# Loading a group's residual among the steps before it, and joining turned planes one sub-step later

## The chip, the cores and the metric

The kernel runs on one core of a Trainium2 chip. The metric is the time of one execution in device microseconds (us). The core has five instruction queues that run beside each other: TensorE (PE: matmuls, and PEld for its weight loads), VectorE (DVE), ScalarE (ACT), GpSimd (POOL) and SyncE (SP), which here issues nearly all DMAs. Each engine takes its instructions strictly in the order in which they were compiled, so an instruction that waits holds up everything behind it on its engine.

## The reference

The input x is 8 sequences of 2048 tokens of 256 features, in fp32. Three residual sublayers follow each other:

```python
x = x + 0.5 * ffn(layernorm(x), w1, b1, w2, b2)
x = x + s4d(layernorm(x), log_A_real, A_imag, C_re, C_im, log_dt, D, ln_w, ln_b)
x = x + 0.5 * ffn(layernorm(x), w1, b1, w2, b2)
```

```python
def ffn(x, w1, b1, w2, b2):              # width 1024
    h = relu(einsum('bsd,dw->bsw', x, w1) + b1)
    return einsum('bsw,wd->bsd', h, w2) + b2

def s4d(x, ...):                         # a long convolution for each of the 256 features
    K = s4d_kernel(log_A_real, A_imag, C_re, C_im, log_dt, length)
    y = irfft(rfft(x) * rfft(K))[:length]
    r = x + y + x * D
    return layernorm(r) * ln_w + ln_b    # over the features
```

The kernel K of the convolution is a sum over 64 complex exponentials for each feature. It depends on the parameters alone, not on x.

## The kernel before

**Stages.** The kernel runs the first feed-forward ("a", up to some 820 us), then the convolution in blocks of 128 tokens (some 820 to 1010 us), then the second feed-forward ("b"). The work that this case is about lies in the first feed-forward. Beside it, the tables of the convolution are computed: the generator `matrices()` makes them, and they need nothing of the feed-forward.

**The feed-forward.** It is cut into 64 groups of 256 tokens, and each group into 8 steps. `sublayer` runs a loop over steps; step t does for group t // 8 one slice of 128 of the 1024 hidden features: six matmuls into the PSUM tile `ph` (`up`, L856; six, because fp32 operands are split into a high and a low part), a relu on ACT that gives the high part (L928), and an instruction on DVE that gives the low part of the same slice (`stt`, recorded as L116, output `hx`). Three steps later (LAG = 3) six matmuls of `down` (L866) add that slice into `po`. So PE needs from ACT and DVE one `hx` for each step. Four `hx` buffers and four `ph` banks lie between them.

**Before a group** (`pre_a`, started 18 steps ahead of its first matmul, one `yield` for each step): its residual is loaded into one of five buffers `x` (L983, one DMA of 256 KB on SP's queue), four steps later (XY = 4) DVE takes its statistics (L693, `st_fa`), ACT normalizes it into `xn` (L730), and it is transposed, either on PE (L794, then ACT L803 and DVE L805) or, in groups 14 to 18 and 44 on, through DRAM by DMA (L815 to L837). Groups 0 to 2 are loaded seven steps later than the others (XL = 7).

**After a group** (`post_a`): DVE adds `po` to the residual (L992), SP stores the result as `x1` (L993), DVE takes its statistics (`st_u`, L693) and ACT writes its normalized form into `u` in two halves (L730, `u`). The statistics of group g are finished together with those of group g + 3 in small instructions of four columns (a `Joint`; `t_u`, `q_u`, `nb_u`, recorded at L714, L116 and L717). The second half of `u` is the last reader of the residual, which then frees its buffer for the load of group g + 5.

**The tables.** `matrices()` ends in a loop over 32 batches; in iteration bt four parts are advanced together through six sub-steps, each part by one `yield` for each sub-step:

- `make(bt)`: POOL computes the batch's matrix P in six instructions of 128x512 (L600 to L610), in one of four buffers, which the batch four before must have left.
- `spread(bt - 1)`: ACT splits P into two planes of 16 bits (L620, two copies), SP stores the planes in DRAM (L623, `pv`) and P itself (L625, `o`).
- `turn(bt - 2)`: SP loads the planes back with a DMA that transposes them (L631).
- `transpose(bt - 3)`: after PY sub-steps the two turned planes are joined to fp32 again, one by DVE and one by ACT (L646, "the join"), in the buffer where P was; a sub-step later SP stores the result (L650, `pt`), and the buffer is free when that store has landed.

There are two buffers of planes, used in turn. The sub-steps are paced beside the steps: a step advances the clock of the feed-forward by 1.32, a sub-step that of the tables by 9.1 / 6 or 10.3 / 6. The work of `lags` (L536 to L570 on POOL, PE and DVE) is advanced in the same loop.

**What sets the order.** The Python code gives an order of calls; a scheduler with a model of time then orders each engine's instructions, except those marked `keep_in_program_order`, which stay in order among themselves. The joins, the turning DMAs and the pinned copies are so marked. A change of one call can therefore move other instructions some places on their engines.

Of the kernel before, what the change touches and what calls it, by code (L numbers as in the profile page):

```python
# [19 lines left out]
P = 128  # L20
# [23 lines left out]
def macaron_s4d_kernel(  # L44
# [17 lines left out]
    nc = tc.nc  # L62
# [4 lines left out]
    B, L, H = x.shape  # L67
# [8 lines left out]
    NTB = 2  # L76
    TOK = NTB * P
    NG = NJ * B // NTB
# [33 lines left out]
    def slot(tag, shape, name, dtype=F32):  # L112
        return work.tile(shape, dtype, name=name, tag=tag, bufs=BUFS[tag])
# [144 lines left out]
    def matrices():  # L258
# [73 lines left out]
        f, a = r, z  # L332
# [29 lines left out]
        for k in range(1, 4):  # L362
# [14 lines left out]
        er, qr, qi, den, ta, tb, c2r, c2i, cr, ci, aa, ab, big, fa, fb, v, s, tt, g, e, mm_ = (  # L377
            cells[18:39]
        )
# [86 lines left out]
        for i in range(H // P):  # L466
            nc.gpsimd.dma_start(
                out=kpad[i * P : (i + 1) * P, P + 1 :], in_=zeros[:, 0 : P - 1]
# [6 lines left out]
        with nc.allow_non_contiguous_dma(reason="256 numbers"):  # L475
            nc.gpsimd.dma_start(
                out=kpad.rearrange("(g c) k -> c g k", c=2)[:, :, P], in_=k0
# [100 lines left out]
        def p_of(bt):  # L578

            r, i = (room[2], 28 + bt % 4 * 8) if bt < first else (room[3], (16, 24, 48, 56)[bt % 4])  # L580
            return r[:, i * P : (i + 8) * P]
# [57 lines left out]
        def transpose(bt):  # L639
            pl, ptb = planes[:, bt % 2], p_of(bt)  # L640
            for _ in range(PY):
                yield
# [9 lines left out]

        planes = wpool.tile([P, 2, 2, BCH * P], U16, name="planes", tag="wE")
        P_REINT = (V.tensor_copy, A_.copy)
        PY = 0
        BACK = 3
        DI = 2
        PX = 2
# [79 lines left out]
    def hbm(ap, g):  # L738
        j, b0 = g // GPJ, g % GPJ * NTB
        return ap[b0 : b0 + NTB, j * P : (j + 1) * P, :].rearrange("b p h -> p b h")  # L740
# [220 lines left out]
    xts = {}  # L961
# [14 lines left out]
    JG = 3  # L976

    def pre_a(g):
        by_dma = g >= DMA_A and not DMA_X <= g < DMA_Y
        for _ in range(XL if g < JG else 0):  # L980
            yield
        xt = xts[g] = slot("x", [P, NTB, H], f"xa_{g}")
        nc.sync.dma_start(out=xt, in_=hbm(x, g))  # L983
        for _ in range(XY):
            yield
        if g >= JG:
            joints[g - JG] = Joint(g - JG, by_dma)
        return (yield from ffn_in(xt, f"a{g}", NTB, by_dma, joints.get(g - JG)))
# [229 lines left out]
    def begin():  # L1218
        for _ in range(sizes[1] // PB):
            next(head)  # L1220

    sublayer(
        w1t, w2t, pre_a, post_a, 18, "a", load_weights(), chain(matrices(), early()),
        {"half": NG // 2, "tables": NG * 3 // 4},
        {NG * SLOTS - 6: lambda: next(head), NG * SLOTS - 1: begin},
# [127 lines left out]
```

## Time and profile before

| | |
|---|---|
| time, median of 3 runs | 1777.33 us (1776.58 to 1781.38) |
| the profiled execution | 1773.09 us, of which its span is 1771.3 us |
| PE busy | 1729.9 us, 98% of the span |
| DVE busy | 1373.3 us, 78% |
| ACT busy | 997.8 us, 56% |
| POOL busy | 591.5 us, 33% |
| joins (L646) | 32 on DVE, median 846 ns, from 248.1 to 602.6 us; 32 on ACT, median 1371 ns |
| residual loads (L983) | 64, 256 KB each, median 3.1 us from issue to landing |
| turning DMAs (L631) | 32, median 5.8 us from issue to landing |

Shares are means over the whole span, and the stages differ. In the rows of the profile, "x" before a number is a count of instructions. A group is named by its line, engine and operation and by what it writes and reads (`hx_a<-ph_a`). A bracket after a row, or a row of the waits, tells how long the engine had stood idle and what ended that. PEclk is the granted share of PE's clock.

### The profile page before, as it was taken

To read this page: it belongs to the slowest core of one execution; us is meant where nothing else is said; L and a number is where in the kernel's file an instruction comes from. 1 tells how busy PE (TensorE), PEld (TensorE's weight loads), DVE (VectorE), ACT (ScalarE), POOL (GpSimd) and SP (SyncE) were. 2 spreads that over 40 slices of the span, in tenths; PEclk is the share of its full clock that TensorE was granted. 3 is DMA by queue.
4 is the path that set the end of the run, shared out by engine and by line. 5 is a ranking of instruction groups with operands and counts; after the bars stand their busy time and mean duration, and the time that the engine had idled before them with its cause. 6 is when DMAs were issued, how large, how long until landed. Compare 5 with 4: busy or idle time off the path is not lost. (4 is left out here: it accounts for less than half of the span.)

```text
span 1771.3 us, 41152 instructions
## 1 busy us (share of the span) xinstructions
PE 1729.9 (98%) x15411; PEld 1701.7 (96%) x15411; DVE 1373.3 (78%) x4415; ACT 997.8 (56%) x2188; POOL 591.5 (33%) x548
## 2 busy tenths in 40 slices
PE   8999999999999999999999899999999999999998
PEld 7999899999999999999999789999999999999998
DVE  6998777677766766766999678887788788888874
ACT  4554567667777755543555445555555555555553
POOL 1116979976776115110000122222222222222220
PEclk9999999999999999999999989999999999999999
DMA  5111266679877643335888913333333333333331
GB/s 194 43 49 40 72 203 209 192 214 288 249 233 238 173 114 94 93 108 170 260 268 260 290 49 90 94 92 91 90 96 96 90 88 93 90 96 96 90 96 49
DMA packets 299407, 245.33 MB, mean 139 GB/s; under 512 B 169924, under 2 KB 242372, under 8 KB 298694
## 3 DMA queue, kind: packets, MB, share of 16 engines
q1 hardware_dynamic: 297456, 241.75, 46.5%
q8 instruction: 121, 1.98, 0.5%
q0 software_dynamic: 768, 0.66, 0.2%
q14 instruction: 80, 0.66, 0.1%
q10 hardware_dynamic: 982, 0.27, 0.1%
HBM read 91.89 MB, written 111.15 MB: 115 GB/s over the span
## 5 line engine op out<-in xcount | busy, mean ns | idle before, releaser
L866 PE MATMUL po_a<-wa,hx_a 128*128 128x256 f32 x3072 | 455.8, 285 | 12.8 <-DVE hx_a L116 12.6
L856 PE MATMUL ph_a<-xh_a,wa 128*128 128x256 f32 x2048 | 455.1, 287 | 1.8 <-ACT xh_a L803 1.4
L856 PE MATMUL ph_b<-xh_b,wb 128*128 128x256 f32 x2048 | 444.9, 285 | 3.5 <-ACT xh_b L803 3.5
L866 PE MATMUL po_b<-wb,hx_b 128*128 128x256 f32 x3072 | 441.3, 283 | 0.1
L866 PEld LDWEIGHTS po_a<-wa,hx_a 128*128 128x128 f32 x3072 | 406.3, 193 | 15.9 <-DVE hx_a L116 15.1
L866 PEld LDWEIGHTS po_b<-wb,hx_b 128*128 128x128 f32 x3072 | 401.0, 192 | 0.3 <-DVE hx_b L116 0.3
L856 PEld LDWEIGHTS ph_a<-xh_a,wa 128*128 128x128 f32 x2048 | 356.1, 193 | 4.9 <-ACT xh_a L803 1.8
L856 PEld LDWEIGHTS ph_b<-xh_b,wb 128*128 128x128 f32 x2048 | 354.4, 194 | 4.1 <-ACT xh_b L803 4.1
L928 ACT ACTIVATE hx_b<-ph_b 128x256 fp32r<-128x256 f32 x512 | 193.8, 383 | 263.6 <-PE ph_b L856 249.6
L928 ACT ACTIVATE hx_a<-ph_a 128x256 fp32r<-128x256 f32 x512 | 192.9, 387 | 212.9 <-PE ph_a L856 206.0
L116 DVE SCALAR_TENSOR_TENSOR hx_a<-ph_a,hx_a 128x256 fp32r<-128x256 f32 x512 | 207.9, 412 | 129.1 <-ACT hx_a L928 127.7
L856 PE MATMUL ph_a<-xl_a,wa 128*128 128x256 f32 x1024 | 291.6, 286 | 3.4 <-DVE xl_a L837 3.1
L856 PE MATMUL ph_b<-xl_b,wb 128*128 128x256 f32 x1024 | 286.4, 285 | 0.0
L116 DVE SCALAR_TENSOR_TENSOR hx_b<-ph_b,hx_b 128x256 fp32r<-128x256 f32 x512 | 211.8, 415 | 66.9 <-ACT hx_b L928 61.5
L1288 POOL TENSOR_TENSOR xb<-xb,lnb_sb 128x512 f32<-128x512 f32 x64 | 82.5, 1292 | 502.1 <-DMA xb<-x_dram 332.4
L856 PEld LDWEIGHTS ph_a<-xl_a,wa 128*128 128x128 f32 x1024 | 198.2, 194 | 4.7 <-DVE xl_a L837 3.7
L856 PEld LDWEIGHTS ph_b<-xl_b,wb 128*128 128x128 f32 x1024 | 198.5, 194 | 0.2 <-DVE xl_b L805 0.2
L777 POOL TENSOR_TENSOR xa<-xa,hb 128x512 f32<-128x512 f32 x64 | 88.9, 1389 | 270.8 <-ACT xn L730 259.6
L777 POOL TENSOR_TENSOR xb<-xb,hb 128x512 f32<-128x512 f32 x64 | 94.6, 1477 | 62.5 <-ACT xn L730 31.8
L730 ACT ACTIVATE xn<-xb,nb_fb,t_fb 128x255 f32<-128x255 f32 x127 | 69.4, 594 | 75.4 <-DVE nb_fb L116 74.2
L815 DVE COPY pl_b<-xn 128x512 uint16<-128x512 uint16 x62 | 39.8, 642 | 74.8 <-ACT xn L730 74.8
L730 ACT ACTIVATE u<-xa,nb_u,t_u 128x256 f32<-128x256 f32 x104 | 89.9, 865 | 0.0
(262 smaller groups left out, 2537.8 us busy)
## 6 DMA issues: line engine op xcount, KB each, us to landing
xa<-in_L_attn_x_dram SPq DMA_DIRECT2D x64, 256.0 KB, 3.1
x_dram<-xa SPq DMA_DIRECT2D x64, 256.0 KB, 2.5
o<-u SPq DMA_DIRECT2D x32, 512.0 KB, 3.6
pv<-planes SPq DMA_DIRECT2D x32, 512.0 KB, 3.5
pt<-u SPq DMA_DIRECT2D x32, 512.0 KB, 3.9
tz<-kpad SPq DMA_DIRECT2D x64, 256.0 KB, 4.5
xb<-x_dram SPq DMA_DIRECT2D x64, 256.0 KB, 2.8
out_dram<-xb SPq DMA_DIRECT2D x64, 256.0 KB, 2.9
```

Of the source, the lines that this page charges most:

```text
L116: return V.scalar_tensor_tensor(out=o, in0=a, scalar=s, in1=b, op0=op0, op1=op1)
L730: ins = A_.activation(dst, src, AF.Identity, bias=nb[:, i : i + 1], scale=rs[:, i : i + 1])
L777: return G_.tensor_add(xt, xt, hb2.unsqueeze(1).to_broadcast([P, NTB, H]))
L815: copy(pl[:, w], xu[:, :, :, :, w])
L856: nc.tensor.matmul(ph, wt[wp][:, dc, fs], xp[:, dc, :], start=(n == 0), stop=(n == 3 * NDC - 1))
L866: nc.tensor.matmul(po[:, i, :], hp[:, tsl], wt[wp][:, fc, :], start=(fc == 0 and i == 0 and n == 0), stop=(fc == NFC - 1 and n == 2), skip ...
L928: last[A_] = A_.activation(hh, ph, AF.Relu)
L1288: G_.tensor_add(xt, xt, lnb_sb.unsqueeze(1).to_broadcast([P, NTB, H]))
```

## The change

Two edits, both in work that runs beside the first feed-forward. In `pre_a` the load becomes a function: groups 0 to 2 still load themselves, and from there on each group loads the one after it, at the point where its own four steps (XY) have passed. And PY, the number of sub-steps that `transpose` lets pass before the join, goes from 0 to 1; the store of `pt` follows the join by one sub-step as before. No instruction is added or left out.

```diff
         planes = wpool.tile([P, 2, 2, BCH * P], U16, name="planes", tag="wE")
         P_REINT = (V.tensor_copy, A_.copy)
-        PY = 0
+        PY = 1
...
         by_dma = g >= DMA_A and not DMA_X <= g < DMA_Y
         for _ in range(XL if g < JG else 0):
             yield
-        xt = xts[g] = slot("x", [P, NTB, H], f"xa_{g}")
-        nc.sync.dma_start(out=xt, in_=hbm(x, g))
+        def load(g):
+            xts[g] = slot("x", [P, NTB, H], f"xa_{g}")
+            nc.sync.dma_start(out=xts[g], in_=hbm(x, g))
+        if g < JG:
+            load(g)
         for _ in range(XY):
             yield
+        xt = xts[g]
+        if JG <= g + 1 < NG:
+            load(g + 1)
         if g >= JG:
             joints[g - JG] = Joint(g - JG, by_dma)
```

## The prediction, before the result was known

> **What bounds the kernel now.** I read the page first, then busy time by stretches, then the waits inside the stretch that the change touches, then single stalls in order of time.
>
> ```profile
> span 1771.3 us, 41152 instructions
> ...
> PE 1729.9 (98%) x15411; PEld 1701.7 (96%) x15411; DVE 1373.3 (78%) x4415; ACT 997.8 (56%) x2188; POOL 591.5 (33%) x548
> ```
>
> TensorE sets the time; a change can only take away or add its idle time. The compiled orders of the two kernels are the same up to the first join (248 us) and again from group 48 on, some 600 us in; later only a few small DVE instructions swap. So I cut there.
>
> ```profile
> core 0: us, PE busy (x) PEld busy (x) DVE busy (x) ACT busy (x) POOL busy (x), PEclk, DMA share, GB/s
> ...
> 315.00:330.00 15.00, 13.70 (x115) 13.49 (x114) 11.80 (x33) 8.98 (x19) 14.91 (x17) 1.00 0.83 218
> ...
> 360.00:410.00 50.00, 44.83 (x350) 44.42 (x349) 38.22 (x87) 32.70 (x61) 37.91 (x33) 0.93 0.69 211
> 410.00:570.00 160.00, 160.00 (x1340) 159.90 (x1339) 111.65 (x328) 123.52 (x233) 114.04 (x97) 1.00 0.83 252
> ...
> 605.00:820.00 215.00, 215.00 (x2028) 212.35 (x2028) 135.32 (x439) 113.44 (x267) 49.73 (x73) 1.00 0.37 106
> ```
>
> Full stretches run 1340/160 = 8.375 matmuls per us, so 360 to 410 is 69 matmuls or 8.2 us short: 5.17 us of idle time and some 3.4 us at a lowered clock (7% of 50 us), two dips of 1.7. From 315 to 330, 1.30 is idle; between the rows 0.28 (352.85) and 0.17 (578.05). About 10 us is all that can be won; 1.81 us at 243.4 lies ahead of the first change.
>
> ```profile
> POOL u L600 <- DMA pt<-u: 29.5, 8, 5.7
> DVE st_fa L693 <- DMA xa<-in_L_attn_x_dram: 23.7, 20, 3.7
> ...
> DVE u L646 <- DMA planes<-pv: 12.4, 9, 3.7
> ...
> PE po_a L866 <- DVE hx_a L116: 8.7, 6, 2.6
> ```
>
> In the waits from 230 to 605 us (total, times, longest) PE waits only for DVE's hx. DVE comes late because it stands before a residual's load (20 times) or a turned plane (9 times). POOL waits for P's buffers, until the stored P (pt) has landed.
>
> ```profile
> 399.63 0.89 DVE L646 COPY u<-planes 128x1024 uint16<-128x1024 uint16 x1 [3.69 <-DMA planes<-pv]
> 400.42 0.67 DVE L992 TENSOR_TENSOR xa<-po_a,xa 128x512 f32<-128x512 f32 x1
> 401.12 0.75 DVE L693 BATCH_NORM_STATS2 st_u<-xa 128x6 f32<-128x256 f32 x2
> 401.79 0.41 DVE L116 SCALAR_TENSOR_TENSOR hx_a<-ph_a,hx_a 128x256 fp32r<-128x256 f32 x1
> ```
>
> ```profile
> 402.25 1.01 PE L866 MATMUL po_a<-wa,hx_a 128*128 128x256 f32 x3 [2.62 <-DVE hx_a L116]
> ```
>
> A late plane in full, in the order of time on DVE and then on PE: DVE stands 3.69 us at the join of batch 12, the copy and three more instructions follow before the next hx, PE loses 2.62. In the same way the joins of batch 6 (wait 2.39, PE 1.30 at 318.0) and 8 (2.35, PE 0.28). The join of batch 11 waits 1.50 and costs PE nothing. So a wait is worth itself less 1.1 to 2.1.
>
> ```profile
> 358.81 6.93 DVE L116 SCALAR_TENSOR_TENSOR q_u<-mv_j,t_u 128x4 f32<-128x4 f32 x1
> ...
> 366.50 0.78 DVE L646 COPY u<-planes 128x1024 uint16<-128x1024 uint16 x1
> ```
>
> The stall of 2.55 at 363.8 is no plane's: a 128x4 instruction, median 0.38 in 29 of this stretch, took 6.93 while POOL ran six tensor instructions from 359.12 to 365.72 without a gap.
>
> **The change, part by part.** *The load.* No DMA and no instruction is added; 60 of 64 loads (0.38 us of SP each, 256 KB, 3.1 to landing) are called four steps earlier, that of group 3 three steps later. A step is 12 matmuls, 1.43 us. But a load still needs its buffer, free after the second u of the group five before: issues at 253.61, 264.66 and 383.92 follow the ends of those u (253.59, 264.64, 383.89) by 0.02 to 0.03. SP's compiled order has the load in nearly the old place: six go just ahead of an x1 store (groups 21, 22, 30, 34, 35, 36), group 23's goes behind a planes store. I cost it at 0; the bounds are -0.17 (the stall at 578, if a load's) and the cost under "join 11" below, where its position counts.
>
> *The join.* 32 DVE copies (846 ns), 32 ACT copies (1371 ns) and 32 pt stores (0.32 us of SP, 3.9 to landing) go one sub-step, about one hx, later. In the compiled DVE order the joins of batches 0 to 4, 6 to 8, 11 and 18 on move by one or two hx, batch 5's comes one earlier, 9, 10 and 12 to 17 stay beside the same hx.
> - Join 6 moves by 1.43: wait 2.39 becomes 0.96, under what costs PE anything: -1.30 (0 to -1.30). Join 8 likewise: -0.28.
> - Join 12 is not moved, but the next hx goes ahead of the two st_u: 0.67 less, PE's gap 1.95. Clock: the gap of 1.81 at 243.4 left it at 1.00, 2.40 at 187.6 and 2.62 here brought 10 us down to a mean of 0.83, a loss of 1.7. At 1.95 I take no dip, being nearer 1.81: -2.38 in all (0 to -4.33).
> - The q_u stall: 2.55 and its dip of 1.7. POOL's order changes just there (L608 between the kpad issues, L600 and L606 ahead of L610), but five independent instructions still stand in a row. Between 0 and -4.26 I take 0.4 of it, -1.70, for a meeting that may or may not recur.
> - Join 11, the added wait. L992 of group 26 now stands behind join 10 on DVE, and on SP the x1 store that needs it stands ahead of the planes store of batch 11. Join 10 ends at 373.4 or so, L992 at 374.1, so that store goes at 374.5 instead of 371.06; with the old 3.8 to landing the transpose goes at 378.3 instead of 374.92 and lands 3.4 later. Queued behind on SP: pt of 10, the transpose, pt of 11. Join 11, itself 1.43 later, waits 3.4 instead of 1.50. By the planes' rows that costs 1.3 to 2.3, but loads' waits of 2.0 to 2.7 cost nothing and one of 3.72 cost 1.81: +1.5 (0 to +4.0, with a dip).
> - Moved ACT copies, transposes on PE (0.28 us each) and statistics trade places in time that is idle on their engines (ACT 123.5 busy of 160): 0; without that cover, one hx, 1.43.
>
> Sum: -1.30 - 0.28 - 2.38 - 1.70 + 1.5 = -4.16. The profiled execution took 1773.09 (span and 1.8 around), 4.24 under the median 1777.33 of the timed runs; it would become 1768.9, the median **1773.2**.
>
> A rule against the -1.7: the Trainium skill, "TensorE: Matmul & The Clock Gate", section "Why this matters for your kernels", asks for no idle gaps over about 3 us. By it no gap here would have lowered the clock, and join 12's term would be -0.67. The rows at 2.40 and 2.62 say otherwise, and the rows decide.
>
> The same skill, "SBUF — State Buffer", section "Who interferes with whom", lets the second of DVE and GpSimd block until the first one's instruction ends: one of 1.30 here, not 6.93. By it the q_u term would be 0, as something else would hold DVE.
>
> **The rivals.**
> 1. *All stalls of the stretch go.* Turned planes land before their joins and q_u misses POOL's run: -1.30 - 0.28 - 4.33 - 4.26 = -10.2, so 1767.2. For it: joins 6, 8 and 12 wait for transposes that the planes' store had held up, and a later join does not delay those. Against: join 12 stays where it is.
> 2. *Slower: the later P feeds back.* From batch 9 on each transpose is issued right after the pt store before it (374.92 after 373.84), and POOL's L600 waits for a pt that landed (370.69). Join 11's 3.4 costs 2.3 and a dip 1.7; its pt is 3.4 later, so is POOL's next L600, the make of 12 queued behind it and that transpose; join 12, unmoved, waits 3.69 + 3.4 - 2.3 = 4.8, PE 1.1 more; with one more dip 1.7 and joins 6 and 8 gained, +5.2: 1782.6. It decides once the planes store of batch 11 goes over 2 us late. Against: from batch 19 on planes land 4 us and more before the join.
> 3. *It does nothing:* loads and transposes keep their pace, stalls merely change place: 1777.3.
>
> **How the numbers follow.** No change can be told within 0.3%, 5.3 us. The sum's case has 0.42, with a range of its own of 1769 to 1777; 0.20 of it lies under 1772.0, 0.22 above. All stalls gone 0.20. Slower 0.33, of which 0.28 over 1782.7 when the chain carries on past batch 12, and 0.05 under. Nothing 0.05. So faster 0.40, same 0.32, slower 0.28. The range goes from 1765 (rival 1 and 2 us of the runs' own spread of 4.8) to 1786 (rival 2 and as much again).
>
> **What would show it.** Right: the stall near 318 gone, joins 6 and 8 waiting under 1 us, loads still issued within 0.1 us of their u, the clock in 398 to 408 back at 1.00. Wrong: DVE's wait at L646 for planes above 12.4 in total, its longest at batch 11, or L600's wait for pt above 29.5 (rival 2); or new hx stalls near 240 to 340, where I found none, from orders of DVE and POOL that I costed at nothing.

## The result, and the profile after

The changed kernel takes 1786.47 us, median of 9 runs (1783.03 to 1791.96), against 1777.06 for the kernel before in the same runs (1775.40 to 1781.38). The ratio is 1.0051, with a 95% interval of 1.0040 to 1.0063: slower by 9.1 us (7.1 to 11.2). The profiled execution took 1785.22 with a span of 1783.4.

The head of the page, changed kernel:

```profile
span 1783.4 us, 41130 instructions
...
PE 1733.7 (97%) x15411; PEld 1703.5 (96%) x15411; DVE 1374.6 (77%) x4415; ACT 995.9 (56%) x2188; POOL 590.9 (33%) x548
```

TensorE executes the same 15411 matmuls, but its span is 12.1 us longer. Where it falls behind is seen in busy time by stretches, changed kernel (each engine's busy time with the number of its instructions, then the granted clock, DMA share and rate):

```profile
246.00:315.00 69.00, 67.59 (x554) 67.39 (x555) 49.63 (x129) 46.87 (x90) 57.95 (x59) 0.98 0.72 216
...
315.00:330.00 15.00, 15.00 (x129) 15.00 (x128) 11.69 (x31) 11.72 (x23) 14.85 (x17) 1.00 0.81 212
...
360.00:410.00 50.00, 43.19 (x352) 42.11 (x352) 35.12 (x88) 32.35 (x62) 39.21 (x37) 1.00 0.70 203
410.00:570.00 160.00, 158.20 (x1310) 156.60 (x1309) 111.97 (x316) 121.56 (x231) 110.96 (x94) 1.00 0.82 241
570.00:580.00 10.00, 7.75 (x65) 7.54 (x63) 5.66 (x21) 3.94 (x9) 5.11 (x5) 1.00 1.02 276
580.00:590.00 10.00, 8.73 (x59) 8.66 (x60) 5.55 (x16) 8.01 (x17) 1.53 (x1) 0.83 0.84 208
590.00:600.00 10.00, 10.00 (x85) 10.00 (x85) 6.37 (x20) 9.11 (x17) 1.54 (x1) 1.00 0.88 189
600.00:625.00 25.00, 23.08 (x186) 22.27 (x185) 15.40 (x52) 16.08 (x33) 3.31 (x3) 1.00 0.56 171
```

Before, 315 to 330 held 115 matmuls and now holds 129: the stall near 318 is gone. From 360 to 410 the clock is back at 1.00 (0.93 before), but new idle time has taken its place (43.19 us busy, 44.83 before), and the row holds 352 matmuls where it held 350. So 16 matmuls or 1.9 us were won from 315 to 410, less than half of what the prediction expected there. Then 410 to 570 was full, with 1340 matmuls, and now holds 1310; and before, the rows below held all or nearly all that fits. Busy time by stretches, kernel before:

```profile
246.00:315.00 69.00, 69.00 (x581) 68.82 (x580) 50.10 (x131) 50.93 (x96) 60.56 (x62) 1.00 0.71 221
...
560.00:600.00 40.00, 39.83 (x332) 39.62 (x331) 26.03 (x84) 33.07 (x65) 11.57 (x9) 1.00 0.81 230
600.00:625.00 25.00, 25.00 (x211) 25.00 (x210) 17.17 (x57) 16.36 (x35) 3.30 (x3) 1.00 0.50 135
```

The four rows of after from 570 to 625 hold 65 + 59 + 85 + 186 = 395 matmuls where 55 us hold 460 at 8.375 per us: 7.8 us lost in a stretch of which the prediction had named nothing. From 410 to 570 another 3.6 us is lost. From 246 to 315 it is 27 matmuls or 3.2 us: 1.04 is a new stall at 274.31, behind VectorE's longest wait for a residual (4.24), and 1.7 a lowered clock behind the stall at 244.33, which stands in the kernel before too (1.81) with no lowered clock.

The waits from 230 to 610 us, changed kernel (total, times, longest):

```profile
DVE st_fa L693 <- DMA xa<-in_L_attn_x_dram: 35.6, 21, 4.2
POOL u L600 <- DMA pt<-u: 32.5, 8, 7.7
...
PE po_a L866 <- DVE hx_a L116: 16.2, 13, 3.5
...
DVE u L646 <- DMA planes<-pv: 11.9, 6, 3.6
...
ACT xf_a L833 <- DMA pt_a<-xp: 5.1, 2, 4.4
DVE xf_a L833 <- DMA pt_a<-xp: 3.4, 2, 2.6
```

The waits for turned planes hardly changed (12.4 before). VectorE's wait for residuals grew from 23.7 to 35.6, and two waits for the DMA transposes of the feed-forward's own planes are there that were not.

The longest stall of TensorE, in the order of the queue. In these rows `o` is the stored P, `pv` P's two planes, `xp` the planes of group 44's normalized input, `pt_a` what the transpose brings back of them; ScalarE makes `xf` and then `xh` of it. First SyncE's issues, changed kernel (start, time of issue):

```profile
565.80 0.32 SPq L650 DMA_DIRECT2D pt<-u  x1
566.21 2.68 SPq L631 DMA_TRANSPOSE planes<-pv  x1
569.00 0.52 SPq L819 DMA_DIRECT2D xp<-pl_a  x1
569.61 0.38 SPq L625 DMA_DIRECT2D o<-u  x1
570.10 0.40 SPq L984 DMA_DIRECT2D xa<-in_L_attn_x_dram  x1
570.74 0.97 SPq L623 DMA_DIRECT2D pv<-planes  x1
571.76 2.06 SPq L823 DMA_TRANSPOSE pt_a<-xp  x1
```

then ScalarE and TensorE in the same place:

```profile
578.55 0.76 ACT L833 COPY xf_a<-pt_a 128x512 uint16<-128x512 uint16 x1 [4.43 <-DMA pt_a<-xp]
579.18 1.33 ACT L646 COPY u<-planes 128x1024 uint16<-128x1024 uint16 x1
...
580.64 0.62 ACT L835 CAST xh_a<-xf_a 128x512 fp32r<-128x512 f32 x1
```

```profile
581.27 0.38 PE L866 MATMUL po_a<-wa,hx_a 128*128 128x256 f32 x1 [3.52 <-DVE hx_a L116]
```

The transpose of group 44 (L823) stands behind a stored P, a residual's load and P's planes, and lands 6.7 us after its issue. It is also issued late: the store of pt (565.80) stood 2.6 us until VectorE's moved join was done, and P's transposing load (566.21), xp and the rest stand behind it. ScalarE waits 4.43 for the transpose, then does P's join (1.33) before the next hx and xh, and TensorE is idle for 3.52. The same queue of the kernel before, around the same transpose:

```profile
561.22 0.34 SPq L819 DMA_DIRECT2D xp<-pl_a  x1
563.27 1.23 SPq L823 DMA_TRANSPOSE pt_a<-xp  x1
```

Here the load (564.59), P's planes (565.18), P's transposing load (569.55) and pt (571.96) are issued behind it. It lands after 3.0, at 566.3, and ScalarE comes to it at 570.36, after the join at 568.88: no wait. The changed kernel's matmuls are some 5.5 us behind at this place and the issue of the transpose 8.5 (571.76 instead of 563.27), so by this estimate it comes 3.0 late by its issue and 3.7 by its landing.

The second new pattern is on VectorE. Timeline near 513, changed kernel:

```profile
513.31 0.16 DVE L116 SCALAR_TENSOR_TENSOR q_u<-mv_j,t_u 128x4 f32<-128x4 f32 x1
517.32 0.75 DVE L693 BATCH_NORM_STATS2 st_fa<-xa 128x6 f32<-128x256 f32 x2 [3.84 <-DMA xa<-in_L_attn_x_dram]
```

and the same group 41 in the kernel before:

```profile
509.43 1.51 DVE L646 COPY u<-planes 128x1024 uint16<-128x1024 uint16 x1
...
511.14 0.75 DVE L693 BATCH_NORM_STATS2 st_fa<-xa 128x6 f32<-128x256 f32 x2
```

Before, the join stood ahead of the residual's statistics (wait 0.15). Now the join is behind them; VectorE comes to the statistics early and stands 3.84, with hx queued behind.

### The profile page after: what moved, and what is told of

It is laid out like the page before. It is cut to its first block, busy times and chain, and to the rows that moved or that the text cites. A ratio compares the mean times of both kernels' runs of the same rounds, so it can differ in the third digit from the quotient of the medians.

```text
span 1783.4 us, 41130 instructions
## 1 busy us (share of the span) xinstructions
PE 1733.7 (97%) x15411; PEld 1703.5 (96%) x15411; DVE 1374.6 (77%) x4415; ACT 995.9 (56%) x2188; POOL 590.9 (33%) x548
## 5 line engine op out<-in xcount | busy, mean ns | idle before, releaser
L815 DVE COPY pl_b<-xn 128x512 uint16<-128x512 uint16 x62 | 44.9, 725 | 74.8 <-ACT xn L730 74.8
```

The source lines that it names most:

```text
L815: copy(pl[:, w], xu[:, :, :, :, w])
```

## The experiments

Below, a gap is a stretch in which TensorE is idle, named by its time in us, with its length in brackets.

**The two edits apart.** First the joins alone.

```diff
-        PY = 0
+        PY = 1
```

> Edit: the joins of P's turned planes one sub-step later, as in the changed kernel; the residuals loaded as in the kernel before. Theory (the join alone makes the loss: ScalarE, VectorE and SyncE take another order of work around it): 8 to 10 us over the kernel before, with the gap of TensorE near 578 (3.5) and those near 504, 518 and 618 still there. Rival (the load edit does it, by its new places on SyncE's queue): no more than 2 us over the kernel before. Rival (only both together): 2 to 5 us over.

Measured: 1.0026 (1.0016 to 1.0036), 4.6 us over the kernel before. The gaps near 571 (3.98), 612 (1.15) and 512 (0.56) are there. So the join alone makes the new stalls, but less time than expected: the theory had left out what it wins earlier. The time alone lies in the range of the last rival (2 to 5).

Then the load edit alone: the changed kernel with `PY = 0`.

> Edit: each residual called for with the steps of the preceding group, as in the changed kernel; the joins where they were before. Theory (a load still waits for its buffer, so the edit does nothing): within 2 us of the kernel before, with its gaps near 318, 364 and 400 still there and none near 578. Rival (the load's new places on SyncE's queue make the loss): 6 to 10 us over. Rival (only both together): within 2 us too, and then the kernel with the joins alone is under 5 us over.

Measured: 1.0013 (1.0001 to 1.0024), 2.3 us over. The gaps near 320 and 366 are there, the one near 400 has shrunk to 0.73; two new ones stand at 572 (1.41) and 575 (0.98), with the clock lowered for 6.8 us. So the load edit does not do nothing.

**The joins by batches,** each in the kernel before, with `PY = 1` in all three.

```diff
-            for _ in range(PY):
+            for _ in range(PY if bt < 12 else 0):
...
-        PY = 0
+        PY = 1
```

> Edit: the kernel before, with only the joins of batches 0 to 11 one sub-step later; the loads stay. Theory (the early joins win what the prediction named near 318 and 400, the load edit alone costs a little): 1 to 4 us under the kernel before, and 1 to 3 under the kernel with early joins and the load edit. Rival (stalls change place and no more): within 1 us of the kernel before.

Measured: 0.9976 (0.9966 to 0.9987), faster by 4.3 us. This version beats both kernels.

```diff
-            for _ in range(PY):
+            for _ in range(PY if 12 <= bt < 26 else 0):
```

> Edit: the kernel before, with only the joins of batches 12 to 25 one sub-step later. Theory (the join stood ahead of the residual's statistics and filled the time until the load landed): TensorE loses 2 to 3 us between 490 and 560 and nothing elsewhere; 1.5 to 3.5 over the kernel before. Rival (these joins are harmless, the loss near 510 comes from what the early joins shifted): within 1 us, and no gap between 490 and 560.

Measured: 1.0017 (1.0005 to 1.0029), 3.0 us over. The timeline of VectorE in this kernel has the wait at group 41 again:

```profile
521.80 0.75 DVE L693 BATCH_NORM_STATS2 st_fa<-xa 128x6 f32<-128x256 f32 x2 [4.08 <-DMA xa<-in_L_attn_x_dram]
...
523.48 0.75 DVE L646 COPY u<-planes 128x1024 uint16<-128x1024 uint16 x1
```

The gap of TensorE beside it is 0.76, less than the 2 to 3 us expected there. That wait is 3.84, 3.81 and 4.08 in the three kernels shown so far whose middle joins are late (changed, joins alone, this one), and 0.00 to 0.81 in those whose middle joins stand where they were (before 0.15; load edit alone 0.40; early joins 0.34). Where the rest of the 3.0 lies can't be read from one profile: this execution also lost 4.5 us between 300 and 410, where its code is that of before.

```diff
-            for _ in range(PY):
+            for _ in range(PY if bt >= 26 else 0):
```

> Edit: the kernel before, with only the joins of batches 26 to 31 one sub-step later. Theory (they put P's pt and planes ahead of the transposes of groups 44 to 46 on SyncE, and themselves between xf and xh): gaps near 575 (over 2.5) and 612 (over 1), 5 to 8 us over the kernel before. With the early joins' 4.2 won and the middle ones' 2 to 3 lost, the parts add up to the 4.6 of all joins. Rival (the place is reached late only because the early joins shifted everything): under 3 us over.

Measured: 1.0044 (1.0026 to 1.0061), 7.8 us over. Busy time by stretches and ScalarE's timeline near 616, this kernel:

```profile
560.00:600.00 40.00, 36.89 (x289) 35.01 (x288) 24.69 (x78) 28.08 (x56) 13.78 (x12) 1.00 0.78 217
600.00:625.00 25.00, 23.13 (x187) 22.32 (x186) 15.47 (x50) 16.06 (x33) 3.30 (x3) 1.00 0.57 163
```

```profile
615.30 0.79 ACT L833 COPY xf_a<-pt_a 128x512 uint16<-128x512 uint16 x1 [2.75 <-DMA pt_a<-xp]
615.95 1.32 ACT L646 COPY u<-planes 128x1024 uint16<-128x1024 uint16 x1
617.14 0.61 ACT L835 CAST xh_a<-xf_a 128x512 fp32r<-128x512 f32 x1
```

Against 332 and 211 before, 43 + 24 = 67 matmuls are missing, 8.0 us; other kernels whose code is unchanged here have 316 to 332, so 1.9 of that may be chance. Near 616 the transpose lands 3.2 us after its issue, as before; ScalarE waits for it because it is issued late. The loss is the last six joins' own and needs no shift by the early ones. Near 575 it comes as several gaps of 0.3 to 0.6, not as one over 2.5. The three parts give -4.3 + 3.0 + 7.8 = +6.5 where all joins together gave 4.6 (2.8 to 6.4).

**The load edit by groups,** each in the kernel with the load edit alone; a group whose load isn't called ahead calls it at the old place. First the groups up to 33 ahead.

```diff
-        if g < JG:
+        if g < JG or g > 33:
             load(g)
...
-        if JG <= g + 1 < NG:
+        if JG <= g + 1 < 34:
```

> Edit: the kernel before, with the load edit for groups up to 33 only. In the compiled order one pair of SyncE's transfers changes places (group 21's load goes ahead of an x1 store), nothing on the other engines. Theory (the load edit's 0.13% lies where it reorders transfers and statistics, from group 30 on): within 1.5 us of the kernel before. Rival (it lies at group 21 and 22, where TensorE stands near 244 and 274): 2 to 4 over, with gaps there longer than 2.1.

Measured: 1.0001 (0.9991 to 1.0010). This swap of two transfers costs nothing that can be measured (-1.6 to 1.8 us).

Then the groups from 34 on.

```diff
-        if g < JG:
+        if g < 34:
             load(g)
...
-        if JG <= g + 1 < NG:
+        if 34 <= g + 1 < NG:
```

> Edit: the kernel before, with the load edit for groups 34 on only. Theory (see the kernel with the loads up to 33): 2 to 4 us over the kernel before, with the idle time of TensorE between 560 and 590 at 2 or more, as with the whole load edit (1.41, 0.98 and a lowered clock). Rival (no loss here, or only one from the clock's windows): within 1.5 us.

Measured: 1.0017 (1.0007 to 1.0028), 3.0 us over, with gaps of 0.77 and 0.99 at 576 and 578. The loss is that of the groups from 34 on. In both kernels with it VectorE waits over 3 for the residual of group 46 (3.51 and 3.15; before 0.90); but the kernel with the early joins alone has 2.89 there too and is the fastest, so this wait is not shown to be the cause. Near 560 and 575 the stores of P and pt also change places on SyncE's queue, which no run takes back alone. The cause stays open.

**The changed kernel with parts taken back.**

```diff
-            for _ in range(PY):
+            for _ in range(PY if bt < 26 else 0):
```

> Edit: the changed kernel, but the joins of batches 26 to 31 at their old sub-step; this puts the transpose of group 44 back directly behind its planes' load on SyncE's queue. Theory (the transposes of groups 44 on are delayed behind P's planes, and the joins of 30 and 31 stand before the xh of their groups): the gaps near 578 (3.52 and a lowered clock worth some 1.7) and 618 (1.50) go, 6.7 us of the changed kernel's loss, so 2 to 4 us over the kernel before. Rival (the loss is spread over groups 30 to 43 by residuals that no join hides any more): at most 2 us of it go, 7 to 9 over the kernel before.

Measured: 1.0014 (1.0006 to 1.0023), 2.5 us over, 6.6 less than the changed kernel. TensorE's longest gap between 560 and 625 is 0.37; from 560 to 600 it holds 314 matmuls, 332 before.

```diff
-            for _ in range(PY):
+            for _ in range(PY if bt < 12 else 0):
```

> Edit: the changed kernel, but only the joins of batches 0 to 11 one sub-step later, the others at their old one. Theory (the loss comes from the joins of batches 18 on): what TensorE loses between 430 and 625 goes, some 8 us of the changed kernel's, and the time is -2 to +2 against the kernel before; the stalls near 318 and 400 stay away, as in the changed kernel. Rival (the slower case of the prediction: batch 11 is late, and the late P feeds back through POOL into all that follow): 8 to 10 us over, as in the changed kernel.

Measured: 1.0001 (0.9991 to 1.0010). No gap stands near 320, the one near 400 is 1.48, none stands between 490 and 560; one of 2.12 stands at 371, with a lowered clock behind it. The join of batch 11 is moved in this kernel too, so the prediction's chain over POOL is not what costs the 9 us.

**The mechanism of the late joins.** In the changed kernel, only the planes of batch 29 leave later; the second pair of lines, after the planes' store, keeps the store of P at its sub-step.

```diff
-            for _ in range(DI):
+            for _ in range(DI + (bt == 29)):
...
-            yield
+            yield from [None] * (bt != 29)
```

> Edit: the changed kernel, but the planes of batch 29 are split and stored one sub-step later, so that on SyncE's queue the transpose of group 44 stands ahead of that store; the joins stay where the change put them (between xf and xh of groups 44 to 46 on ScalarE). Theory (in the changed kernel the transpose lands 6.7 us after its issue, not 3.0 as before, because P's planes go out just ahead of it): it lands in 3 to 4.5, the gap of TensorE near 578 falls from 3.52 to under 1 with no lowered clock behind it, the one near 618 stays: 3 to 5 us under the changed kernel, 4 to 6 over the kernel before. Rival (the join between xf and xh on ScalarE, or the transpose's late issue, makes the gap): it stays over 2.5, and so does the changed kernel's time.

Measured: 1.0034 (1.0021 to 1.0048), 6.0 us over. SyncE, ScalarE and TensorE near 576, this kernel:

```profile
570.19 1.25 SPq L823 DMA_TRANSPOSE pt_a<-xp  x1
```

```profile
575.85 0.78 ACT L833 COPY xf_a<-pt_a 128x512 uint16<-128x512 uint16 x1 [2.74 <-DMA pt_a<-xp]
576.50 1.32 ACT L646 COPY u<-planes 128x1024 uint16<-128x1024 uint16 x1
577.69 0.60 ACT L835 CAST xh_a<-xf_a 128x512 fp32r<-128x512 f32 x1
```

```profile
578.35 0.50 PE L856 MATMUL ph_a<-xh_a,wa 128*128 128x256 f32 x2 [1.51 <-ACT xh_a L835]
```

The transpose lands after 5.6, better than 6.7 but not the 3.0 to 4.5 expected; a stored P and a load still go ahead of it, and it lands 2.7 after the later of the two (573.07). The gap falls from 3.52 to 1.51, not under 1, and a window of lowered clock still follows (579.33). So what goes just ahead of the transpose does act. But from 560 to 600 this kernel holds 298 matmuls, the changed kernel 290 and the one before 332: 1.0 us of some 5 comes back. What is left is the rival's: the transpose is still issued late, and TensorE now waits for xh, with the join (1.32) between xf and xh on ScalarE. No run takes either of these away alone, so their shares aren't shown. The gain against the changed kernel is 3 us by the two ratios, whose intervals overlap.

**The mechanism of the middle joins.** In the changed kernel, the residual's statistics one step later.

```diff
         if joint:
+            yield
             stats(halves(xt), f"f{name}", mv=joint.mv[:, 0:NTB])
-            for _ in range(joint.norm_at):
+            for _ in range(joint.norm_at - 1):
```

> Edit: the changed kernel, but in groups 3 on the statistics of the residual are taken one step later (the normalisation stays at its step). Theory (the later joins no longer fill VectorE's time until a residual has landed, and hx stands behind the statistics): VectorE's wait for residuals between 230 and 610 falls from 35.6 to under 20, the gaps near 504 and 518 and the one near 244 go: 3 to 6 us under the changed kernel, 4 to 7 over the kernel before. Rival (the statistics are needed just then, so that square root and normalisation come later): the waits move to ScalarE and TensorE, and the time is the changed kernel's or more.

Measured: 1.0061 (1.0049 to 1.0073), 10.8 us over, no better than the changed kernel. No wait for a residual is left from 230 to 610 (35.6 before this edit), and busy time by stretches is full where the changed kernel held 92 and 102 matmuls:

```profile
500.00:512.00 12.00, 12.00 (x103) 12.00 (x103) 9.08 (x25) 8.75 (x17) 10.57 (x10) 1.00 0.75 235
512.00:525.00 13.00, 13.00 (x111) 13.00 (x110) 9.05 (x28) 9.34 (x19) 9.47 (x9) 1.00 0.78 241
```

So the loss there is VectorE's wait for residuals. But with the later statistics other gaps grow: there are some of 3.17 at 155, 3.47 at 365, 3.21 at 402 and 2.93 at 618, each with a lowered clock behind it. The same edit on top of the faster version:

> Edit: as the kernel with early joins and the loads of before, and also the residual's statistics one step later. Theory (residual loads hold VectorE, 23.7 us of waits from 230 to 605 before): the gap of TensorE near 244 (1.8 to 2.0, with a lowered clock in some executions) goes and the waits for residuals fall under 12: 2 to 5 us under that kernel, 4 to 8 under the kernel before. Rival (the statistics' chain is due at that step): no better than that kernel.

Measured: 0.9992 (0.9980 to 1.0005). The gap near 244 is gone, those near 155 (3.15), 365 (3.00) and 401 (2.59) are longer. Statistics one step later are no better with either set of joins.

## Why the prediction was wrong

The sign was wrong: 1773.2 was forecast, with 1765 to 1786 as the range, and 1786.5 came.

- *The priced terms came out in total, not one by one.* They were joins 6, 8, 11 and 12 and the q_u stall, all before 410 us, and gave -4.16. The early joins alone measured -4.3 us (-6.0 to -2.3). But in that kernel's profile join 12's gap is 2.44 where 1.95 was priced, with no lowered clock; q_u's is 1.72 with a lowered clock; and join 11 costs nothing. That these errors cancel is partly luck.
- *In the changed kernel* join 6's stall is gone. Join 12 still waits (3.55), but TensorE's gap is 1.56 and no clock is lowered, a little more than was priced. The q_u meeting recurs: its second instruction takes 4.91 beside four tensor instructions of POOL in a row, where the first took 6.93 beside six; the gap is 1.77 instead of 2.55, with no lowered clock, 2.5 won instead of 1.70. *Join 11's added wait* was placed wrongly: it waits 0.78; join 10 waits 3.64 instead and costs 2.91, more than the 1.5 taken and within its 0 to 4.0. With other small gaps, 1.9 us is left of the 4.16.
- *The step that failed* is the last item of the list: "Moved ACT copies, transposes on PE (0.28 us each) and statistics trade places in time that is idle on their engines (ACT 123.5 busy of 160): 0; without that cover, one hx, 1.43". It stood for every moved join without a term of its own, the 14 of batches 18 to 31 among them. The joins of batches 12 to 25 measured +3.0 (0.9 to 5.2), those of 26 to 31 +7.8 (4.6 to 10.8). Idle time in the mean says nothing on what stands directly ahead of what: the join had been filling VectorE's wait for a load, and on ScalarE it stood, after the change, between xf and xh. And pt's later store was counted for POOL, not for the transpose of group 44 behind it on the same queue. The remark that from batch 19 on planes land 4 us and more before the join (batch 26: 1.5) says only that these joins don't wait, not what waits for them.
- *The load edit at 0* failed too. That a load still needs its buffer was right: with the load edit alone 43 of 59 loads are issued within 0.1 us of its release, 41 before, 37 in the changed kernel. But from some 430 us on transfers change places on SyncE's queue, and statistics and small instructions on VectorE's; the loss of 2.3 (0.2 to 4.3) goes with the groups from 34 on. What in it costs the time stays open.
- *Rival 2* had the sign and nearly the size (1782.6), but another place and cause. POOL's wait for pt is 32.5 in the changed kernel, 8.7 in the one with the joins alone, which is slower too, and 38.2 in the fastest version: it doesn't go with the time. The prediction's own test "L600's wait above 29.5" would have named the wrong cause. Its other sign, new hx stalls near 240 to 340, did come, with the 1.04 at 274, in the changed kernel and with neither edit alone; no run explains it.
- The parts add up within their intervals, each of which is 2 to 3 us to either side: -4.3 + 3.0 + 7.8 for the joins and +2.3 for the loads give 8.8, all joins at once (4.6) with the loads 6.9; measured was 9.1 (7.1 to 11.2).

## What to carry to other kernels

When one constant moves a step that occurs many times, price each occurrence by what stands next to it on its engine and on its queue, not a few of them by their waits and the others by mean idle time; here the joins of the first 12 batches won 4.3 us and the rest lost 10.8. A step that stands ahead of a wait may be filling it for nothing, and moving it away brings the wait to light. Then split the edit by occurrences: applying it only where it won gave a version faster than both kernels (0.9976).

## What the runs showed of the hardware

**The clock is granted by fixed windows.** In all 14 profiles the lowered stretches start a whole number of 3.41 us apart. Cutting each profile between 100 and 1000 us into such windows, every one of the 42 windows in which TensorE was idle for 1.9 us or more was followed by one at half clock (a loss of 1.7 us); of those with 0.9 to 1.45 idle, none was, unless it ran at half clock itself; between the two it went both ways. The half of a window, 1.7, lies between. So it depends on where a gap falls: kernel before, the windows around the stalls at 399.6 and 243.4 (granted clock: the third number from the right):

```profile
398.34:401.75 3.41, 1.29 (x11) 1.09 (x10) 2.08 (x4) 2.12 (x4) 3.17 (x4) 1.00 0.75 273
401.75:405.16 3.41, 2.91 (x13) 2.91 (x14) 3.41 (x13) 0.30 (x1) 3.33 (x3) 0.50 0.99 294
241.33:244.74 3.41, 1.94 (x15) 1.53 (x13) 3.27 (x11) 1.23 (x4) 3.41 (x4) 1.00 0.76 262
244.74:248.15 3.41, 2.95 (x23) 2.88 (x24) 2.37 (x6) 0.85 (x3) 3.26 (x5) 1.00 0.80 244
```

and the changed kernel, where a gap of 2.91 at 375.73 falls on two windows and costs no clock, and one of 2.04 at 244.33 in a single window does:

```profile
373.60:377.01 3.41, 2.13 (x18) 1.92 (x17) 1.19 (x2) 1.95 (x4) 3.07 (x3) 1.00 1.13 342
377.01:380.43 3.42, 1.79 (x15) 1.79 (x16) 3.39 (x15) 1.17 (x5) 3.42 (x4) 1.00 0.66 261
380.43:383.84 3.41, 3.41 (x31) 3.41 (x30) 2.09 (x7) 2.32 (x6) 2.45 (x3) 1.00 0.74 223
243.89:247.30 3.41, 1.37 (x11) 1.17 (x10) 3.31 (x6) 0.80 (x2) 3.41 (x5) 1.00 0.81 178
247.30:250.71 3.41, 3.41 (x18) 3.41 (x17) 1.58 (x4) 1.66 (x5) 3.04 (x4) 0.50 0.39 150
```

The prediction took the gap's length as the rule ("at 1.95 I take no dip"), which is not what decides. The Trainium skill, "TensorE: Matmul & The Clock Gate", section "What's actually happening", has the window of 3413 ns and says that it runs freely; the first agrees with these rows, and so does the second, as the windows fall elsewhere in the span from one profile to the next. It asks for an idle window before the clock falls; here about half a window was enough.

**A transpose landed later behind transfers still under way.** The same transposing DMA of group 44 landed after 3.0 us with nothing but its own store, already landed, ahead of it; after 5.6 behind a stored P and a load; and after 6.7 behind a stored P, a load and P's planes issued in the 2.2 us before. In the last two it landed 2.7 and 2.5 after the last of them. Their number alone doesn't decide: the changed kernel's transpose at 600.69 had three under way ahead of it, too, and landed after 3.7.

**One profile is good to a few microseconds per stretch.** In the kernels with only middle or only last joins late, the gap near 320 was 2.30 where before had 1.30, in code that was the same. The timed ratios, not the stretches of one profile, carry the prices above.
